# Inverse square root of the layer norms by Newton steps on VectorE, in a four-layer graph network

## The chip, the cores and the metric

The kernel runs on one core of a Trainium2 chip. A core has five engines that work side by side, each through its own instruction queue in order: TensorE (PE in the profile, with its weight loads as PEld), VectorE (DVE), ScalarE (ACT), GpSimd (POOL) and SyncE (SP, which here only starts transfers). They wait for each other by semaphores. The metric is the time of one execution on the device, in microseconds; several runs are made and their median is given. One further execution was recorded by the hardware profiler, and every view of the profile is of that one.

## The reference

Four layers run over 4096 nodes of 128 features and a 4096 x 4096 matrix `adj` that is mostly zero. Each layer first normalizes the rows and clips them at zero, computes a graph operation and adds the result to the rows.

```python
def _layernorm(x, axis=-1, eps=1e-5):
    m = jnp.mean(x, axis=axis, keepdims=True)
    v = jnp.var(x, axis=axis, keepdims=True)
    return (x - m) / jnp.sqrt(v + eps)

h = jnp.maximum(_layernorm(x, axis=-1), 0.0)
x = x + _L0_gnn_ref(h, adj, L0_gnn_W, L0_gnn_b)
h = jnp.maximum(_layernorm(x, axis=-1), 0.0)
x = x + _L1_gnn_ref(h, adj, L1_gnn_weight, L1_gnn_bias)
h = jnp.maximum(_layernorm(x, axis=-1), 0.0)
x = x + _L2_gnn_ref(h, adj, L2_gnn_weight, L2_gnn_att_src, L2_gnn_att_dst)
h = jnp.maximum(_layernorm(x, axis=-1), 0.0)
x = x + _L3_gnn_ref(h, adj, L3_gnn_msg_w, L3_gnn_msg_b, L3_gnn_upd_w, L3_gnn_upd_b, L3_gnn_ln_w, L3_gnn_ln_b)
```

The layers numbered 0 to 3 are these. Layer 0 multiplies by `adj` once and by two weights. Layer 1 multiplies by `adj` twice (a Chebyshev recursion). Layer 2 is an attention with `exp` over the nonzero places of `adj`. Layer 3 sends a message through a GELU for every nonzero place, sums the messages of a row weighted by `adj`, applies an update with another GELU and then a second layer norm of its own:

```python
        h = jax.nn.gelu(new_feats, approximate=False) + node_feats
        mu = jnp.mean(h, axis=-1, keepdims=True)
        var = jnp.var(h, axis=-1, keepdims=True)
        return (h - mu) / jnp.sqrt(var + LN_EPS) * ln_w + ln_b
```

## The kernel before

The rows lie in 32 blocks of 128 (a block is one row per partition), and four blocks make a group: there are eight groups, `NC`. The matrix is used as a list: the kernel reads `adj` once, marks its nonzero places (`mark`, a Sigmoid on ScalarE into an 8-bit mask), scans the masks on VectorE (`scan`), and builds lists of the rows and columns that each stripe of 256 needs. Blocks near the front of the ordering are dense and are multiplied as they are; the rest is gathered by indirect DMAs that GpSimd issues (`gather`, L552-L554). `entries` decodes the single nonzero places for layer 3.

The order of all this isn't written by hand. Every part is a Python generator that yields what it will need next: an engine with an estimated duration (`yield "DVE", 0.35`), a buffer from a set of slots, or an event. `Plan.run` picks, again and again, the part that could begin first, lets it emit its instructions and advances a clock for that engine. An activation that names a table (`on_act(n, "sqrt")`) costs 1.3 us more in the plan when the table last named was another one. At the end `in_order` fixes the order in which each engine's instructions came out. So an estimate that changes moves what stands beside it in all five queues. Gaps on TensorE which the plan foresees are filled with products of zeros (`fill`, L604-L610).

The layer norm in front of each layer is `norm` (L557-L580). It takes a `stat` tile with four rows of small numbers. VectorE sums each block's rows and scales the sum to minus the mean (L563, L564); ScalarE squares the centred rows with an accumulator, one block at a time, into a scrap tile `junk` (L568); ScalarE takes the square root of the variance plus `eps` (L572); VectorE takes the reciprocal and multiplies by minus the mean (L574, L575); ScalarE applies scale, bias and Relu block by block (L578). `norm` is called from four places: `begin` for two groups at a time (four calls with eight blocks each), `finish_0` and `finish_2` after layers 0 and 1 (eight calls each, four blocks), and `finish_3` after the attention (eight calls). That makes 28.

Layer 3's own norm is in `Messages.finish` (L1428-L1471), called once for each group. After the update's matmuls (L597) VectorE adds the bias (L1441), ScalarE applies the GELU (L1444), and VectorE adds the rows and forms the mean (L1447-L1449). Then come the same steps as in `norm`: squares (L1453), square root (L1456), reciprocal and product (L1458, L1459), and four Identity activations that scale the four blocks (L1462). VectorE multiplies by `ln_w` and adds the rows (L1466, L1467), and the group is stored. `ln_b` has been added to the rows earlier, at L1392.

Beside it in stage order, the parts that share the engines with these steps are: in the attention, `attend`, where ScalarE forms scores (L1229) and their `exp` (L1232), VectorE multiplies them by the matrix twice (L1236, L1238) and TensorE accumulates (L1253, L1255); in layer 2's preparation an `exp` of two columns (L1042); in layer 3, `prepare`, which runs a group's own rows through a GELU (`own`, L1377) and opens the group's sum (L1386), and `message`, where ScalarE and VectorE build a selection (L623, L625), VectorE a weight mask (L1403), TensorE the message's two terms (L1409, L1411), ScalarE its GELU (L1415), and TensorE adds it to the group's sum (L1421).

A second program, `dense_stack`, is there for matrices that the lists can't hold. It is behind a condition that does not hold for these inputs.

Of the kernel before, what the change touches and what calls it, by code (L numbers as in the profile page):

```python
# [18 lines left out]
I32 = mybir.dt.int32  # L19
AF = mybir.ActivationFunctionType  # L20
ALU = mybir.AluOpType
# [5 lines left out]
D = 128  # L27
P = 128
# [3 lines left out]
GB = BANK // D  # L32
HALF = N // 2
QUARTER = N // 4
EPS = 1e-5
# [331 lines left out]
def on_act(n, table=None):  # L367
    return ("ACT", 0.22 + 0.83e-3 * n) + ((table,) if table else ())
# [10 lines left out]
def sparse_stack(tc, x, adj, adjT, diag, w_self, w_neigh, b0, w1, b1, w2, att_src, att_dst,  # L379
# [7 lines left out]
    nc = tc.nc  # L387
    plan = Plan()
    EARLY = 7
    with ExitStack() as ctx:  # L390
# [7 lines left out]
        def kept(name, shape, dtype=F32):  # L398
            return keep.tile(list(shape), dtype, name=name, tag=name)
# [46 lines left out]
        nc.gpsimd.memset(ones, 1.0)  # L446
        ones8 = kept("ones8", (P, 1), F8)
        nc.gpsimd.memset(ones8, 1.0)
        eps = kept("eps", (P, 1))
        nc.gpsimd.memset(eps, EPS)  # L450

        def iota(name, shape, pattern, base=0, step=0, dtype=F32):
            t = kept(name, shape, dtype)
# [100 lines left out]
                                         in_offset=bass.IndirectOffsetOnAxis(ap=index, axis=0))  # L554


        def norm(blocks, dst):  # L557

            n = blocks.stop - blocks.start
            st = yield stats  # L560
            src = xN[:, blocks, :]
            yield on_dve(n * D)
            nc.vector.tensor_reduce(st[:, 0, :n], src, axis=AX.X, op=ALU.add)  # L563
            nc.vector.tensor_scalar_mul(st[:, 0, :n], st[:, 0, :n], -1.0 / D)  # L564
            junk = yield junks
            yield "ACT", 0.58 * n
            for k in range(n):
                nc.scalar.activation(junk, src[:, k, :], AF.Square, bias=st[:, 0, k:k + 1],  # L568
                                     accum_out=st[:, 1, k:k + 1])
            plan.release(junks, junk)  # L570
            yield on_act(n, "sqrt")
            nc.scalar.activation(st[:, 1, :n], st[:, 1, :n], AF.Sqrt, bias=eps, scale=1.0 / D)  # L572
            yield "DVE", 0.35
            nc.vector.reciprocal(st[:, 2, :n], st[:, 1, :n])  # L574
            nc.vector.tensor_mul(st[:, 3, :n], st[:, 0, :n], st[:, 2, :n])  # L575
            yield "ACT", 0.45 * n
            for k in range(n):
                nc.scalar.activation(dst[:, k, :], src[:, k, :], AF.Relu, scale=st[:, 2, k:k + 1],  # L578
                                     bias=st[:, 3, k:k + 1])
            plan.release(stats, st)  # L580
# [736 lines left out]
        class Messages:  # L1317
# [110 lines left out]
            def finish(self, g):  # L1428
                blocks = slice(g * GB, (g + 1) * GB)
                plan.release(s_tiles, self.s_rows[g])  # L1430
                agg = yield aggs
                yield on_act(BANK)
                nc.scalar.copy(agg, self.acc[g])
                plan.release(accs if g else picks, self.acc[g])
                p = yield banks
                yield "PE", 8 * 0.42
                times(p, GB, [(hT[:, g * BANK:(g + 1) * BANK], upd_h_sb), (agg, upd_a_sb)])
                plan.release(aggs, agg)
                f = yield f_tiles
                yield on_dve(BANK)  # L1440
                nc.vector.tensor_tensor(f, rows_of(p), by_block(upd_b_sb, GB), op=ALU.add)  # L1441
                plan.release(banks, p)
                yield on_act(BANK, "gelu")
                nc.scalar.activation(f, f, AF.Gelu)  # L1444
                st = yield stats
                yield "DVE", 1.5
                nc.vector.tensor_add(f, f, hA[:, blocks, :])  # L1447
                nc.vector.tensor_reduce(st[:, 0, :GB], f, axis=AX.X, op=ALU.add)
                nc.vector.tensor_scalar_mul(st[:, 0, :GB], st[:, 0, :GB], -1.0 / D)  # L1449
                junk = yield junks  # L1450
                yield "ACT", 0.58 * GB
                for k in range(GB):
                    nc.scalar.activation(junk, f[:, k, :], AF.Square, bias=st[:, 0, k:k + 1], accum_out=st[:, 1, k:k + 1])  # L1453
                plan.release(junks, junk)
                yield on_act(GB, "sqrt")
                nc.scalar.activation(st[:, 1, :GB], st[:, 1, :GB], AF.Sqrt, bias=eps, scale=1.0 / D)  # L1456
                yield "DVE", 0.35
                nc.vector.reciprocal(st[:, 2, :GB], st[:, 1, :GB])  # L1458
                nc.vector.tensor_mul(st[:, 3, :GB], st[:, 0, :GB], st[:, 2, :GB])  # L1459
                yield "ACT", 0.45 * GB  # L1460
                for k in range(GB):
                    nc.scalar.activation(f[:, k, :], f[:, k, :], AF.Identity, scale=st[:, 2, k:k + 1],  # L1462
                                         bias=st[:, 3, k:k + 1])
                plan.release(stats, st)
                yield "DVE", 1.4
                nc.vector.tensor_mul(f, f, by_block(ln_w_sb, GB))  # L1466
                nc.vector.tensor_add(f, f, xN[:, blocks, :])  # L1467
                yield SP
                nc.sync.dma_start(out_rows[:, blocks, :], f)
                plan.release(f_tiles, f, plan.transfer(P * BANK * 4) - 1)  # L1470
                self.through.set(plan.finish)  # L1471
# [526 lines left out]
```

## Time and profile before

| | |
|---|---|
| time, median of 3 runs | 1176.93 us (1172.99 to 1178.95) |
| the profiled execution, its own time | 1485.49 us |
| the profiled execution, span | 1483.4 us |
| mean granted TensorE clock in it | 0.842 |
| instructions | 19188 |
| moved by DMA | 236.03 MB, mean 159 GB/s |
| Square activations in `norm` (L568) | 128, 401 ns each |
| square roots (L572, L1456) | 36, 297 ns each |
| reciprocals (L574, L1458) | 32 with 128x4 elements, 173 and 178 ns each |
| Identity activations (L1462) | 32, 479 ns each |
| Relu activations (L578) | 128, 479 to 482 ns each |

The profiled execution is longer than the timed runs by 309 us, so a position in it (a microsecond from the start of the span) is not a position in a timed run. What can be carried over are durations of single instructions and the order in each queue, which is the same in every run.

A group of instructions in the profile is named by its line, engine and operation, and by what it writes and reads. After the bar stand the busy time and the mean duration of one in nanoseconds, and after the second bar the idle time of the engine just before them. Mean durations are given with start to end; neighbours overlap a little, so the distance from start to start can be smaller. In the chain of waits each entry has its start, its length and what ran: an engine with tile and line, or "issue" where the engine waited for nothing that the profile shows.

### The profile page before, as it was taken

How to read it: one execution, taken by the hardware profiler on the slowest of the kernel's cores; microseconds unless marked ns; L12 is line 12 of the kernel's file. 1: busy time of each engine (PE TensorE's matmuls, PEld its weight loads, DVE VectorE, ACT ScalarE, POOL GpSimd, SP SyncE). 2: the span in 40 equal slices, each digit the busy share in tenths (PEclk: the TensorE clock that was granted, in tenths of full speed). 3: DMA queues.
4: the chain of work that ended last, by engine and by line, in shares of the span. 5: the costliest groups of instructions: out<-in, count | busy, mean ns of one | idle time of the engine just before them, and what ended most of it. 6: DMA issues, size and time to landing. Idle time of an engine off the chain costs nothing.

```text
span 1483.4 us, 19188 instructions
## 1 busy us (share of the span) xinstructions
PE 1055.1 (71%) x5943; PEld 722.2 (49%) x5943; DVE 792.7 (53%) x2982; ACT 671.2 (45%) x1344; POOL 766.4 (52%) x832
## 2 busy tenths in 40 slices
PE   6786778877486687667677069968767872957774
PEld 2454556554265465455555045534434452645663
DVE  5796567787466476345645048444444451424453
ACT  5983466664021213113335048656555630334366
POOL 4136664344635565546656733765557346664530
PEclk9897799897697899778888579979888995988988
DMA  8999899895565777766544034333333212112210
GB/s 252 357 329 334 286 299 330 305 353 185 135 185 147 211 228 227 201 187 181 150 115 132 8 93 132 107 88 89 88 107 97 61 50 49 42 42 53 61 45 24
DMA packets 175415, 236.03 MB, mean 159 GB/s; under 512 B 22452, under 2 KB 155336, under 8 KB 167112
## 3 DMA queue, kind: packets, MB, share of 16 engines
q1 hardware_dynamic: 148904, 186.45, 37.8%
q0 software_dynamic: 26400, 48.27, 13.6%
q8 instruction: 49, 0.80, 0.2%
q14 instruction: 62, 0.51, 0.1%
HBM read 203.41 MB, written 31.23 MB: 158 GB/s over the span
## 4 chain that ended last, share of the span: by engine, by line
PE 23%; another core or an unknown queue 13%; ACT 10%; DVE 7%; issue 6%; DMA 1%; POOL 0%; ACTq 0%; SPq 0%; DVEq 0%; POOLq 0%
PE acc L1253 4%; PE acc L1255 3%; PE bank L597 2%; PE acc L1421 2%; PE acc L1139 2%; PE acc L1156 2%; ACT junk L1453 1%; ACT e L1229 1%; ACT junk L568 1%; PE bank L1411 1%; PE pick L610 1%; ACT e L1232 1%; PE bank L1409 1%; DVE ehit L891 1%
## 5 line engine op out<-in xcount | busy, mean ns | idle before, releaser
L553 POOL DMA_INDIRECT e_val<-in_adj,e_at x158 | 154.5, 978 | 48.0 <-issue 45.6
L553 POOL DMA_INDIRECT g<-h_tab,fetch_row x136 | 136.1, 1001 | 73.0 <-issue 34.3
L610 PE MATMUL pick<-nothing 128*128 128x512 f16 x536 | 142.9, 416 | 1.6 <-issue 1.6
L1139 PE MATMUL acc<-big,hA 128*128 128x256 f32 x448 | 131.7, 442 | 10.7 <-issue 7.7
L610 PEld LDWEIGHTS <-nothing 128*128 128x128 f16 x795 | 82.9, 107 | 99.3 <-issue 33.4
L553 POOL DMA_INDIRECT g<-a_tab,fetch_col x74 | 76.9, 1039 | 93.6 <-issue 45.3
L553 POOL DMA_INDIRECT rseg<-in_adjT,seg_row x68 | 71.1, 1046 | 103.4 <-issue 28.8
L1139 PEld LDWEIGHTS acc<-big,hA 128*128 128x128 f32 x448 | 96.4, 225 | 28.6 <-issue 9.5
L553 POOL DMA_INDIRECT cseg<-in_adj,seg_col x74 | 70.8, 957 | 63.9 <-issue 23.2
L891 DVE SCALAR_TENSOR_TENSOR ehit<-ehit,pos,pick 128x32 f32<-128x32 f32 (+7 forms) x158 | 38.8, 285 | 116.0 <-issue 80.1
L1236 DVE TENSOR_TENSOR tau<-e,big 128x512 f32<-128x512 f32 (+3 forms) x61 | 54.3, 891 | 85.5 <-ACT e L1232 47.8
L553 POOL DMA_INDIRECT g<-u_tab,fetch_row x68 | 64.6, 950 | 64.9 <-PE acc L1156 37.1
L888 ACT COPY ehit<-pick 128x192 f32<-128x192 f32 (+7 forms) x74 | 20.4, 286 | 154.5 <-remote 80.4
L553 POOL DMA_INDIRECT tau<-d_tab,e_col x63 | 60.6, 962 | 57.2 <-issue 15.0
L769 ACT ACTIVATE mask<-dst 128x2048 fp8e4<-128x2048 f32 x43 | 81.8, 1903 | 14.2 <-DMA dst<-in_adj 8.0
L553 POOL DMA_INDIRECT m<-d_tab,e_col x70 | 68.4, 977 | 38.5 <-issue 17.4
L1156 PE MATMUL acc<-big,g 128*128 128x256 f32 x272 | 80.2, 434 | 0.6 <-DMA big<-r_tab 0.5
L568 ACT ACTIVATE junk<-xN,stat 128x128 f32<-128x128 f32 x128 | 51.4, 401 | 60.0 <-DVE stat L564 27.0
L623 ACT ACTIVATE sel_t<-iota_row,mids 128x512 f32<-128x512 f32 (+3 forms) x43 | 27.1, 642 | 109.7 <-DVE mids L618 63.7
L610 PE MATMUL bank<-nothing 128*128 128x512 f16 x259 | 70.6, 414 | 2.7 <-issue 2.3
L884 PE MATMUL pick<-eA,esel 128*128 128x65 f16 (+7 forms) x158 | 27.0, 245 | 61.4 <-DVE esel L625 28.0
L1139 PE MATMUL acc<-big,hB 128*128 128x256 f32 x224 | 62.7, 420 | 1.7 <-DMA big<-in_adjT 1.7
(331 smaller groups left out, 2717.2 us busy)
## 6 DMA issues: line engine op xcount, KB each, us to landing
dst<-in_adj SPq DMA_DIRECT2D x43, 1024.0 KB
big<-in_adjT SPq DMA_DIRECT2D x45, 512.0 KB
raw<-in_adj SPq DMA_DIRECT2D x21, 1024.0 KB
big<-in_adjT SPq DMA_DIRECT2D x66, 256.0 KB
big<-r_tab SPq DMA_DIRECT2D x30, 512.0 KB
c_tab<-cseg SPq DMA_DIRECT2D x74, 128.0 KB
r_tab<-rseg SPq DMA_DIRECT2D x68, 128.0 KB
big<-c_tab SPq DMA_DIRECT2D x15, 512.0 KB
```

The costliest lines, as they stand in the source:

```text
L553: nc.gpsimd.indirect_dma_start(out=dst, out_offset=None, in_=table[:, :], in_offset=bass.IndirectOffsetOnAxis(ap=index, axis=0))
L568: nc.scalar.activation(junk, src[:, k, :], AF.Square, bias=st[:, 0, k:k + 1], accum_out=st[:, 1, k:k + 1])
L597: nc.tensor.matmul(p[:, k * D:(k + 1) * D], lhs[:, k * P:(k + 1) * P], w, start=i == 0, stop=i == len(terms) - 1)
L610: nc.tensor.matmul(idle[2][idle[1]], nothing[:, :P], nothing, start=True, stop=True)
L769: nc.scalar.activation(mask[:, h * HALF:(h + 1) * HALF], raw_of[b, h], AF.Sigmoid, scale=1e38, accum_out=marks[:, 2 * b + h:2 * b + h + 1] ...
L891: nc.vector.scalar_tensor_tensor(hit[:, q, :], hit[:, q, :], pos0[:, k + q:k + q + 1], pv[:, q, W:2 * W], op0=ALU.is_le, op1=ALU.mult, acc ...
L1139: nc.tensor.matmul(acc, self.near[:, b, :D], as_rows(t)[:, k, :], start=count == 0, stop=count == every - 1)
L1156: nc.tensor.matmul(acc, row[:, :D], r, start=count == 0, stop=count == every - 1)
L1236: nc.vector.tensor_mul(tau[:, :n, :], e[:, :n, :], a[:, :n, :])
L1253: nc.tensor.matmul(acc[0:1, CS:2 * CS], parts[k][:, D + 1:], tau[:, k, :], start=False, stop=False)
L1255: nc.tensor.matmul(acc[:, :CS], parts[k][:, :D], e[:, k, :], start=False, stop=self.count[s.index] == every - 1)
L1421: nc.tensor.matmul(acc[:, b % GB * P:(b % GB + 1) * P], m[:, q, :], r[:, q, :], start=False, stop=all(self.left[g * GB + k] == 0 for k in ...
```

## The change

`norm` and `Messages.finish` no longer take a square root on ScalarE and a reciprocal on VectorE. A new function `inverse_root` computes the inverse square root on VectorE alone: one operation for the variance plus `eps`, a shift and a subtraction on the number's bits for a first guess, and three Newton steps of three operations each. These are twelve operations on tiles of 128x4 (128x8 in `begin`), and each needs the result of the one before. The product with minus the mean that followed stays. In the planner's terms a step "ACT" with the table "sqrt" and a step "DVE" of 0.35 us become one step "DVE" of 1.6 us. The constant `eps` and its memset go.

In `Messages.finish` the first two of a group's four blocks are scaled by ScalarE as before, and the last two by VectorE with a `tensor_scalar` of the same two operands.

```diff
--- before.py
+++ after.py
@@ -446,8 +446,6 @@
         nc.gpsimd.memset(ones, 1.0)
         ones8 = kept("ones8", (P, 1), F8)
         nc.gpsimd.memset(ones8, 1.0)
-        eps = kept("eps", (P, 1))
-        nc.gpsimd.memset(eps, EPS)
 
         def iota(name, shape, pattern, base=0, step=0, dtype=F32):
             t = kept(name, shape, dtype)
@@ -554,6 +552,17 @@
                                          in_offset=bass.IndirectOffsetOnAxis(ap=index, axis=0))
 
 
+        def inverse_root(st, n):
+
+            v, y, t = (st[:, k, :n] for k in (1, 2, 3))
+            nc.vector.tensor_scalar(v, v, 1.0 / D, EPS, op0=ALU.mult, op1=ALU.add)
+            nc.vector.tensor_scalar(y.bitcast(I32), v.bitcast(I32), 1, None, op0=ALU.logical_shift_right)
+            nc.vector.tensor_scalar(y.bitcast(I32), y.bitcast(I32), -1.0, float(0x5f3759df), op0=ALU.mult, op1=ALU.add)
+            for _ in range(3):
+                nc.vector.scalar_tensor_tensor(t, y, -0.5, y, op0=ALU.mult, op1=ALU.mult)
+                nc.vector.tensor_mul(t, t, v)
+                nc.vector.scalar_tensor_tensor(y, t, 1.5, y, op0=ALU.add, op1=ALU.mult)
+
         def norm(blocks, dst):
 
             n = blocks.stop - blocks.start
@@ -568,10 +577,8 @@
                 nc.scalar.activation(junk, src[:, k, :], AF.Square, bias=st[:, 0, k:k + 1],
                                      accum_out=st[:, 1, k:k + 1])
             plan.release(junks, junk)
-            yield on_act(n, "sqrt")
-            nc.scalar.activation(st[:, 1, :n], st[:, 1, :n], AF.Sqrt, bias=eps, scale=1.0 / D)
-            yield "DVE", 0.35
-            nc.vector.reciprocal(st[:, 2, :n], st[:, 1, :n])
+            yield "DVE", 1.6
+            inverse_root(st, n)
             nc.vector.tensor_mul(st[:, 3, :n], st[:, 0, :n], st[:, 2, :n])
             yield "ACT", 0.45 * n
             for k in range(n):
@@ -1452,15 +1459,17 @@
                 for k in range(GB):
                     nc.scalar.activation(junk, f[:, k, :], AF.Square, bias=st[:, 0, k:k + 1], accum_out=st[:, 1, k:k + 1])
                 plan.release(junks, junk)
-                yield on_act(GB, "sqrt")
-                nc.scalar.activation(st[:, 1, :GB], st[:, 1, :GB], AF.Sqrt, bias=eps, scale=1.0 / D)
-                yield "DVE", 0.35
-                nc.vector.reciprocal(st[:, 2, :GB], st[:, 1, :GB])
+                yield "DVE", 1.6
+                inverse_root(st, GB)
                 nc.vector.tensor_mul(st[:, 3, :GB], st[:, 0, :GB], st[:, 2, :GB])
-                yield "ACT", 0.45 * GB
-                for k in range(GB):
+                yield "ACT", 0.45 * (GB // 2)
+                for k in range(GB // 2):
                     nc.scalar.activation(f[:, k, :], f[:, k, :], AF.Identity, scale=st[:, 2, k:k + 1],
                                          bias=st[:, 3, k:k + 1])
+                yield "DVE", 0.3 * (GB // 2)
+                for k in range(GB // 2, GB):
+                    nc.vector.tensor_scalar(f[:, k, :], f[:, k, :], st[:, 2, k:k + 1], st[:, 3, k:k + 1],
+                                            op0=ALU.mult, op1=ALU.add)
                 plan.release(stats, st)
                 yield "DVE", 1.4
                 nc.vector.tensor_mul(f, f, by_block(ln_w_sb, GB))
```

## The prediction

> **What bounds the kernel now.** I read the page's totals first, then each engine by stage, then ScalarE's groups, then the chain of work that ended last. The totals and the stages:
>
> ```profile
> PE 1055.1 (71%) x5943; PEld 722.2 (49%) x5943; DVE 792.7 (53%) x2982; ACT 671.2 (45%) x1344; POOL 766.4 (52%) x832
> ...
> 0.00:412.00 412.00, 302.52 (x2184) 194.50 (x2185) 286.66 (x932) 238.85 (x395) 193.82 (x244) 0.85 0.84 285
> 412.00:882.00 470.00, 309.45 (x1581) 240.13 (x1579) 241.90 (x1342) 122.92 (x300) 270.93 (x287) 0.81 0.56 161
> 882.00:1184.00 302.00, 244.99 (x1053) 135.15 (x1054) 142.41 (x301) 190.18 (x395) 162.08 (x158) 0.89 0.35 96
> ```
>
> The stage rows give start:end, length, then the busy time of PE, weight loads, DVE, ACT and POOL, the clock, the DMA share and GB/s. I call them A (layer 0, the scan of the matrix), B (layers 1 and 2), C (attention) and D (messages, from 1184 to the end). In A the DMA engines are 84% busy: transfers set the pace. No engine fills B to D; there the order of waits decides.
>
> ScalarE's groups, shapes kept apart, show where its function tables are loaded:
>
> ```profile
> L572 ACT ACT_TABLE_LOAD x26 | 33.4, 1283 | 0.5
> L769 ACT ACT_TABLE_LOAD x10 | 12.8, 1283 | 0.2
> L1232 ACT ACT_TABLE_LOAD x8 | 10.3, 1283 | 0.1
> L1456 ACT ACT_TABLE_LOAD x8 | 10.3, 1283 | 0.1
> L1042 ACT ACT_TABLE_LOAD x7 | 9.0, 1283 | 0.1
> L1377 ACT ACT_TABLE_LOAD x6 | 7.7, 1283 | 0.1
> ```
>
> With three at L1415 and one each at L1444 and L1482 there are 70 loads of 1283 ns: 89.8 us, 13% of ScalarE's busy time. 34 are the square roots' own (L572, L1456); most others bring back the table that a square root displaced.
>
> The chain in D, at one `finish` (start, length, what):
>
> ```profile
> 1411.07 0.49 ACT junk L1453 x2
> 1411.56 0.02 issue
> 1411.58 1.28 ACT L1456
> 1412.86 0.01 issue
> 1412.88 0.30 ACT stat L1456
> 1413.17 0.02 issue
> 1413.19 1.28 ACT L1377
> 1414.47 0.01 issue
> 1414.48 0.64 ACT own L1377
> 1415.12 0.04 issue
> 1415.17 2.08 PE acc L1386 x8
> ```
>
> An ACT entry with a line and no tile is a table load. The next group's GELU (`own`, L1377) needs nothing of this square root; it stands behind it in ScalarE's order, and TensorE waits for it. Load, root and reload cost that path 1.30 + 0.32 + 1.30 = 2.92 us with their issue gaps.
>
> I added up such entries over the whole chain, which this view resolves from 579 us on (none in A). A load begun as 0.04 plus "issue" of about 1.2 counts as one. B: 6 loads, 7.7 us. C: 12 loads, 15.0 us. D: 16 loads, 20.4 us. Together 43 us.
>
> **What the Trainium skill says.** *ScalarE: Activation LUTs*, What ACT_TABLE_LOAD costs: 1283 ns a load for every set, plus about 1380 ns of drain. The 1283 is the trace's to the nanosecond; the drain is not: the root starts 1.29 us after its load starts, so I price a load at 1.30. The same page, Table sets: sqrt, exp, sigmoid and gelu anchor different sets, relu, copy, abs and identity are in every one. The trace agrees: no load stands at the Relu (L578), the copies (L590) or the Abs (L623). *VectorE: DVE Perf Modes*, The TRN2 errata: a fixed cost per instruction, for a float32 two-tensor operation (N+151)/0.96 ns; for 4 elements an estimate of 161 ns, and L1459 took 163. *SBUF — State Buffer*, Who interferes with whom: VectorE operations with two SBUF inputs or in a two-port mode lock a port that GpSimd shares[...]. All twelve new operations are of these kinds; the trace speaks on both sides, below.
>
> **The change part by part.**
>
> *Removed from ScalarE.* 36 square roots (28 at L572, 8 at L1456) of 0.297 us: 10.7 us. The loads: after the change only sigmoid, exp and gelu need tables, and these come nearly in this order by stage. I keep one each, a return to exp after the first early GELU in C, and a few alternations: 6 to 10 of 70. So about 62 loads or 79.5 us go. The 16 identities that leave L1462 (0.385 us from start to start) are 6 us. ACT falls from 671 to about 575.
>
> *Added to VectorE.* Twelve operations for each of 36 norms, each needing the one before. A dependent chain of such small operations runs at 0.213 us per step with POOL idle:
>
> ```profile
> 658.32 0.18 DVE L922 TENSOR_TENSOR da<-da,db 128x22 int32<-128x22 int32 x1
> 658.53 0.18 DVE L921 TENSOR_SCALAR db<-dv 128x22 int32<-128x22 int32 x1
> 658.75 0.18 DVE L922 TENSOR_TENSOR da<-da,db 128x22 int32<-128x22 int32 x1
> 658.96 0.18 DVE L921 TENSOR_SCALAR db<-dv 128x22 int32<-128x22 int32 x1
> ```
>
> 12 x 0.213 = 2.56 us, against the reciprocal's 0.21: 2.35 us more a norm, 85 us of the queue's time in all (some 70 busy). DVE goes from 793 to about 867, the 16 moved blocks at 0.28 included. Where the norm's own result is waited for, the path had 1.30 + 0.32 + 0.21 = 1.83 and gets 2.56: 0.73 us longer.
>
> *D.* Three chain passages go through `own` as above: 3 x 2.92 = 8.8. Three go through the scaling (L1462), which began 3.45 us after the last `junk` (1328.55 to 1332.00). It can now begin after 2.56 + 0.21 = 2.77, and ScalarE does two blocks in 0.87 instead of four in 1.63: 3 x (0.68 + 0.76) = 4.3. At 1465 the last GELU (L1444) stands behind load, root and reload: 2.92. The last norm loses 0.73 and gains 0.76 in its scaling: nothing. One root of a norm at 1196 gives 1.6. Sum 17.6. The two blocks on VectorE lie beside ScalarE's two; without that cover they cost 0.56. What is behind the twelve operations on DVE: masks and selections of the next messages (L1403, L625), for which TensorE waits at L1421 and L1411. DVE is 43% busy there and covers them; uncovered they cost 8 x 2.35 = 19 us.
>
> *C.* 15.0 + 5 roots at 0.32 = 16.6 if all comes off. But after the loads at 955, 1072 and 1149 the chain runs into waits of 16.0, 11.7 and 9.3 us which the profile gives to an unknown queue. Time saved ahead of such a wait may only lengthen it. Bounds 0 and 16.6; I take half, 8.3. Behind the twelve operations stand the products of the attention (L1236, L1238) that feed L1253 and L1255.
>
> *B.* 7.7 + 0.3, less 2.35 where the norm at 893 is followed by its own use: 5.7. After three of the five loads at L1042 an unknown wait follows (6.6, 15.1, 2.4 us). Bounds 0 and 5.7; I take 2.5.
>
> *A.* 22 loads and 12 roots, 32 us of ScalarE, lie under the DMA. Only at the start (17 to 35 us) was ScalarE busy without a break ahead of the first mask, so the reads start up to 2.9 us sooner: I take 2. DVE gets 28 us more on 287 of 412; if that holds up the scan it costs, so bounds 8 won and 8 lost.
>
> *Sum.* 17.6 + 8.3 + 2.5 + 2 = 30.4; I give back 5 for what queues behind the DVE blocks (bounds 0 and 36, the blocks of C and D all uncovered): 25 us. The removed `eps` constant is one small memset on POOL: nothing. The planner lays out all five queues anew from the changed costs, so neighbours move everywhere; I add no mean for that, only spread, some 10 us either way (a choice, not a reading).
>
> **Against the profile's own time.** The profiled execution took 1485.49 us, its span 1483.4, which leaves 2.1 around it; with the change it would take about 1460. The timed runs' median is 1176.93, 309 less. The chain's unknown waits and issue from 579 on come to 198 + 95 us, near that, but nothing shows that they are the difference. The loads have one fixed duration, so I carry the 25 us over in microseconds: 1152.
>
> **The rivals.**
>
> *All of it counts.* If the unknown waits are shorter in timed runs, B and C come off whole: 17.6 + 16.6 + 5.7 + 8 and 4 for a better order in D, 52 us: 1125. For it: the 309 us. Against it: TensorE is 81% busy in C.
>
> *Absorbed.* The waits of B and C end where they ended, and the DVE blocks eat most of D: 3 us remain, 1174. For it: the waits that follow the loads. Against it: the passages of D, where TensorE waits for ScalarE directly.
>
> *VectorE's chain stalls on POOL (slower).* In one burst of gathers small operations were held for a gather's period of 1.25 us each:
>
> ```profile
> 817.60 0.16 DVE L848 SCALAR_TENSOR_TENSOR middle<-efirst,half 128x4 f32<-128x4 f32 x1 [1.08 <-DVE half L847]
> 818.99 0.17 DVE L849 TENSOR_TENSOR mids<-middle,shift 128x12 f32<-128x12 f32 x1 [1.23 <-DVE middle L848]
> ```
>
> A norm there costs 12 x (1.25 - 0.213) = 12.4 us more. It decides from two norms on the path (25 / 12.4); with four it gives 1152 + 50 = 1202. Against it: from 695 to 700 POOL was 75% busy and a like chain still took 0.21 us a step.
>
> **How the numbers follow.** Forecast 0.50 (own range 1137 to 1166), all of it 0.20, absorbed 0.17, stall 0.13. A measurement here can tell about 0.5%, 6 us, from none. Faster: 0.50 + 0.20 + 0.07 of the absorbed case = 0.77; same 0.10; slower 0.13. The range 1122 to 1182 leaves out the stall's upper part and the far end of the second case, under 0.2 in all.
>
> **What would show it.** Right: 6 to 10 loads in all and none behind a `junk`, ACT near 575 and DVE near 867, `own` following `junk` at once in D, and a norm's twelve steps in about 2.6 us. Wrong: those steps spread over 5 us or more, TensorE waiting for L1403, L625 or L1236 behind them, or the unknown waits of C longer by what was saved.

## The result, and the profile after

The change made a difference of a few us at most: 1176.22 us against 1177.15 us for the kernel before (medians of 20 runs each on one chip), ratio 0.9983, 95% interval 0.9963 to 1.0003. A second comparison, on another chip, gave 1174.98 us against 1178.90, ratio 0.9972 (0.9948 to 0.9996). The forecast of 1152 us was wrong; "absorbed", at 1174, came nearest. Medians here and below are of all runs, while ratios and their intervals leave out runs well above the fastest of the same kernel, so that the two can differ by some tenths of a per cent.

One fact has to stand ahead of every reading. There are chips on which the kernel before took 1470 to 1555 us in every run, with mean granted TensorE clocks of 0.816 to 0.845. The profile that the prediction read (1485.49 us, clock 0.842) looks like one of these, though which chip it came from isn't on record; the times are from chips on which the kernel takes 1177 us. All profiles below are of the second kind unless the text says otherwise, and so the kernel before is shown here from a profile of its own there (span 1175.5 us).

The page of the changed kernel, totals and slices (a slice is 29.5 us):

```profile
PE 986.2 (84%) x5853; PEld 677.7 (57%) x5853; DVE 863.2 (73%) x3394; ACT 575.7 (49%) x1228; POOL 773.1 (66%) x831
...
PE   5888787888788898888888879889999978778783
...
DVE  6799898878878887675898866666567672356785
ACT  4985556655522212231434456577677642234552
POOL 5127746545437677777777777777777777777770
```

The same of the kernel before, on a chip of the same kind:

```profile
PE 985.6 (84%) x5943; PEld 675.0 (57%) x5943; DVE 792.2 (67%) x2982; ACT 673.5 (57%) x1344; POOL 769.7 (65%) x832
...
PE   5977988898788888787898789898999988887892
...
DVE  5789988889878758567877756465546482455563
ACT  4997667676523131231556486477778761255676
POOL 5115777435546777777777778777777747777760
```

And the POOL row of the page that the prediction had before it:

```profile
POOL 4136664344635565546656733765557346664530
```

ScalarE lost 98 us of work and VectorE gained 71, as forecast, and neither shows in the time. Look at POOL. From the fourteenth slice on both rows say 7 almost throughout, and 7 looks like slack. It isn't. A gather is recorded for 0.94 us, the next begins 0.30 us after its end for "issue", and 0.94 of 1.25 is 7 tenths: a row of sevens is a full queue. In the third row there are sixes, fives, fours and threes, pauses that this kernel has only on the other kind of chip.

TensorE's share needs a caution too. It includes the products of zeros with which the plan fills gaps (L610 before, L617 after): 208 of the 985.6 us before and 185 of the 986.2 us after.

ScalarE's groups in the changed kernel hold all table loads that are left, six, one to a line; two of them:

```profile
L776 ACT ACT_TABLE_LOAD x1 | 1.3, 1283 | 0.0
L1049 ACT ACT_TABLE_LOAD x1 | 1.3, 1283 | 0.0
```

VectorE's timeline at one norm of `finish_3`, changed kernel (start, length):

```profile
952.52 0.19 DVE L558 TENSOR_SCALAR stat<-stat 128x4 f32<-128x4 f32 x1
952.76 0.17 DVE L559 TENSOR_SCALAR stat<-stat 128x4 int32<-128x4 int32 x1
952.97 0.19 DVE L560 TENSOR_SCALAR stat<-stat 128x4 int32<-128x4 int32 x1
953.20 0.16 DVE L562 SCALAR_TENSOR_TENSOR stat<-stat 128x4 f32<-128x4 f32 x1
...
955.00 0.16 DVE L582 TENSOR_TENSOR stat<-stat 128x4 f32<-128x4 f32 x1
```

Twelve operations from 952.52 to 955.00 are 2.48 us; 2.56 had been worked out. Over all 36 norms of this profile they take 2.37 to 2.62 us. The single operations of the Newton steps take 164 ns (L562 to L564, 96 of each at four elements), where 161 had been estimated. The parts of the change were priced right. What bounds the kernel was not.

**Where the time lies.** GpSimd's gathers come in the same number in every kernel that keeps them (595 after the last gather of row segments, `rseg`), so they serve as marks. I cut the span at the start of that last `rseg` gather and at the first gather of `tau`, the message rows that need the attention's result complete: its last part must have been stored in the table `d_tab` first. GpSimd's timeline, kernel before:

```profile
350.78 0.95 POOL L553 DMA_INDIRECT rseg<-in_adjT,seg_row  x1 [0.30 <-PE pick L657]
...
956.37 0.93 POOL L553 DMA_INDIRECT e<-d_tab,e_col  x1 [0.30 <-ACT junk L568]
968.48 0.95 POOL L553 DMA_INDIRECT tau<-d_tab,e_col  x1 [11.18 <-DVE n_bad L1524]
...
1142.00 0.92 POOL L553 DMA_INDIRECT e<-d_tab,e_col  x1 [0.30 <-issue]
```

The changed kernel:

```profile
365.17 0.95 POOL L551 DMA_INDIRECT rseg<-in_adjT,seg_row  x1 [0.30 <-PE pick L664]
...
928.41 1.26 POOL L551 DMA_INDIRECT g<-a_tab,fetch_col  x1 [0.30 <-issue]
929.98 0.94 POOL L551 DMA_INDIRECT e_val<-in_adj,e_at  x1 [0.30 <-DVE e_val L953]
...
943.93 0.95 POOL L551 DMA_INDIRECT e_val<-in_adj,e_at  x1 [0.30 <-issue]
...
969.34 0.94 POOL L551 DMA_INDIRECT e<-d_tab,e_col  x1 [0.30 <-issue]
970.59 0.94 POOL L551 DMA_INDIRECT tau<-d_tab,e_col  x1 [0.30 <-issue]
...
1148.92 0.92 POOL L551 DMA_INDIRECT e<-d_tab,e_col  x1 [0.31 <-issue]
```

The brackets give the idle time before the entry and what ended it. So part 1 (A and a little less) ends at 350.8 and 365.2 us, part 2 (B and C) lasts 617.7 and 605.4 us, part 3 (D) 207.0 and 209.0 us. The prediction's profile, cut the same way, has 387.3, 820.6 and 275.5: of the 308 us between it and the kernel before at 1177 us, 271 lie in parts 2 and 3.

In part 2 the kernel before has a pause of 11.2 us at its end; the changed one has none. In both, some 33 us pass from the attention's last gather (`g<-a_tab`, at 932.8 before and 928.4 after) to the start of the last store into `d_tab` (965.6 and 962.3), which must land before `tau`. The old order left 18 gathers for that stretch, 22 us of GpSimd's work. The new one leaves 32, since twelve gathers of edge values, which the old order had put earlier, now stand after the attention's last gather. So the attention's gathers are also served sooner: its last one starts 582 us after the last `rseg` before, 563 us after it now.

A second profile of the changed kernel (span 1165.9 us) has 350.9, 606.6 and 208.5. The 13.7 us between the two lie in part 1 alone; parts 2 and 3 differ by 0.6 us in sum over some 815 us. I use that as a tool: the sum of parts 2 and 3 is read from one profile, and part 1, which scatters, is the median time less that sum (some 2 us around the span included). That the sum repeats so well rests on this one pair; on the slower chips three profiles of the kernel before have 1085, 1096 and 1104 us.

### The profile page after: what moved, and what is told of

It is laid out like the page before. It is cut to its first block, busy times and chain, and to the rows that moved or that the text cites. A ratio compares the mean times of both kernels' runs of the same rounds, so it can differ in the third digit from the quotient of the medians.

```text
span 1179.6 us, 19316 instructions
## 1 busy us (share of the span) xinstructions
PE 986.2 (84%) x5853; PEld 677.7 (57%) x5853; DVE 863.2 (73%) x3394; ACT 575.7 (49%) x1228; POOL 773.1 (66%) x831
## 5 line engine op out<-in xcount | busy, mean ns | idle before, releaser
L551 POOL DMA_INDIRECT e_val<-in_adj,e_at x158 | 159.1, 1007 | 48.0 <-issue 41.6
L1146 PE MATMUL acc<-big,hA 128*128 128x256 f32 x448 | 121.1, 413 | 3.0 <-DMA big<-in_adjT 3.0
L617 PEld LDWEIGHTS <-nothing 128*128 128x128 f16 x705 | 71.8, 104 | 79.8 <-issue 19.8
L617 PE MATMUL pick<-nothing 128*128 128x512 f16 x435 | 117.5, 417 | 0.0
L1146 PEld LDWEIGHTS acc<-big,hA 128*128 128x128 f32 x448 | 88.1, 207 | 15.4 <-DMA big<-in_adjT 3.8
L551 POOL DMA_INDIRECT m<-d_tab,e_col x79 | 78.4, 992 | 24.1 <-issue 13.7
L1163 PE MATMUL acc<-big,g 128*128 128x256 f32 x272 | 75.0, 407 | 7.6 <-DMA big<-r_tab 4.4
L551 POOL DMA_INDIRECT tau<-d_tab,e_col x67 | 66.7, 996 | 20.4 <-issue 11.9
L617 PE MATMUL bank<-nothing 128*128 128x512 f16 x270 | 67.1, 385 | 0.0
L1163 PE MATMUL acc<-rseg,g 128*128 128x256 f32 x136 | 51.9, 490 | 13.1 <-DMA g<-h_tab,fetch_row 13.1
L1163 PEld LDWEIGHTS acc<-big,g 128*128 128x128 f32 x272 | 50.9, 200 | 18.8 <-issue 7.9
```

Of the source, the lines that this page charges most:

```text
L551: nc.gpsimd.indirect_dma_start(out=dst, out_offset=None, in_=table[:, :], in_offset=bass.IndirectOffsetOnAxis(ap=index, axis=0))
L617: nc.tensor.matmul(idle[2][idle[1]], nothing[:, :P], nothing, start=True, stop=True)
L1146: nc.tensor.matmul(acc, self.near[:, b, :D], as_rows(t)[:, k, :], start=count == 0, stop=count == every - 1)
L1163: nc.tensor.matmul(acc, row[:, :D], r, start=count == 0, stop=count == every - 1)
```

## The experiments

**On a chip like that of the first profile.** Four kernels ran on one of the slower chips, where the kernel before takes 1483.12 us (median of 23). The kernel before once more:

> The kernel before once more, for a profile beside which the changed kernel's can be laid (its own profile had a span of 1483 us, the changed one's 1180). Theory (GpSimd's queue): GpSimd issues its 736 gathers without a pause from about 400 us on, one each 1.25 us, and the last one starts between 1140 and 1155 us, as in the changed kernel (1149); the table loads are there (70) and hidden beside it. Rival (the gain was given back on VectorE): here GpSimd has pauses of more than 20 us in sum after 400 us, and waits for ScalarE show in the chain.

1470.12 us, span 1468.1: the profile that was predicted from is no outlier there. The theory failed on this chip: after the last `rseg` GpSimd pauses for some 260 us in sum, as the rival said.

The kernel before and the changed kernel, each without the 158 gathers of edge values (the values that layer 3's messages take from the matrix are left out):

```diff
-                        gather(e_val[:n, k:k + 1], adj_flat, e_at[:n, k:k + 1])
```

> The kernel before, the order of all other instructions held, without the 158 gathers of matrix values (the values of layer 3's messages are left out, their weights are zero). Theory (GpSimd's queue): 158 x 1.25 = 197 us leave the queue that sets the time, so the time falls by 60 to 197 us, until something else is the bound. Rival (VectorE gave the gain back; GpSimd is not the bound): within 15 us of the kernel before.

> The changed kernel, the order of all other instructions held, without the same 158 gathers (the values of layer 3's messages are left out). Theory (GpSimd's queue): falls as the kernel before does without them, and now that GpSimd no longer covers it the change shows: 8 to 30 us faster than the kernel before without them. Rival (given back on VectorE): the two are within 5 us of each other, or this one is slower.

1335.39 us, ratio 0.9042 (0.8961 to 0.9122), and 1330.36 us, 0.8988 (0.8926 to 0.9051). Some 150 us go in both, and without these gathers the two still differ by no more than 5 us, which is what the rival said and not the theory. More gathers, 28 of them issued twice into the same place, in the changed kernel:

```diff
                         gather(e_val[:n, k:k + 1], adj_flat, e_at[:n, k:k + 1])
+                        if number >= 5 and k % 3 == 0:
+                            gather(e_val[:n, k:k + 1], adj_flat, e_at[:n, k:k + 1])
```

> The changed kernel with 28 of its value gathers (those of the later row groups, issued after about 550 us) issued twice, everything else in the same order. Theory (GpSimd's queue): 28 x 1.25 = 35 us more in a queue without pauses, so 25 to 35 us slower. Rival: under 10 us slower, since GpSimd is busy for 66% of the span and has room.

1496.38 us, ratio 1.0074 (1.0044 to 1.0105) to the kernel before, 11 us more, which lies nearer the rival (the changed kernel wasn't run there without the doubled gathers). Little can be concluded from this chip for the 1177 us, but gathers weigh there too.

**The parts of the change, on chips with 1177 us.** The changed kernel again:

> The changed kernel once more, beside the kernel before and the other runs of this call on one chip. On the chip of the last call the kernel before took 1483 us instead of 1177. Theory (gathers on GpSimd, or what waits for them, set the time; ScalarE's loads lie beside them): ratio to the kernel before 0.985 to 1.005 wherever it runs. Rival (the prediction's path of loads counts where the chip is the slower one): 0.965 to 0.985 there.

1174.98 us, as above; on this chip the kernel before takes 1178.90. Then the loads alone, on the same chip: the kernel before in its old order, with an Identity where the square root stood and nothing added to VectorE (the root itself is left out; the same edit is made in `Messages.finish`):

```diff
-            nc.scalar.activation(st[:, 1, :n], st[:, 1, :n], AF.Sqrt, bias=eps, scale=1.0 / D)
+            nc.scalar.activation(st[:, 1, :n], st[:, 1, :n], AF.Identity, bias=eps, scale=1.0 / D)
```

> The kernel before in its own order, with the square root activation replaced by an Identity of the same size (the root is left out, the rows are scaled by the reciprocal of the variance): no square root table, so about 64 of the 70 loads go, and VectorE gets nothing in return. Theory (loads lie beside the gathers): less than 10 us faster. Rival 1 (the loads were on the path and VectorE's twelve operations gave the gain back): 20 to 45 us faster. Rival 2 (the new order gave it back): also 20 to 45 us faster.

1165.36 us against 1178.90, ratio 0.9855 (0.9796 to 0.9914): 64 of the 70 loads are worth 13.5 us by the medians, 10 to 24 by the interval (four runs). That is more than the theory allowed, by the median less than both rivals asked for, and less than the 30.4 that had been added up. Then the twelve operations in the old order, with the old durations left in the plan and all four scalings on ScalarE (the same edit in `Messages.finish`):

```diff
             yield on_act(n, "sqrt")
-            nc.scalar.activation(st[:, 1, :n], st[:, 1, :n], AF.Sqrt, bias=eps, scale=1.0 / D)
             yield "DVE", 0.35
-            nc.vector.reciprocal(st[:, 2, :n], st[:, 1, :n])
+            inverse_root(st, n)
```

> The twelve operations on VectorE in place of root and reciprocal, but with the planner's old estimates, so that every queue keeps the order of the kernel before (the scaling of the blocks is unchanged). Theory: within 8 us of the kernel before. Rival 1 (VectorE gives it back): within 8 us too, but then noload_before is 20 us or more faster than this. Rival 2 (the new order cost what the loads gave): 15 to 40 us faster than the kernel before and than the changed one.

1181.01 us, ratio 1.0017 (0.9997 to 1.0036). The same order with loads off and operations on is 15.6 us slower than with loads off alone. So in the old order the operations take back what the loads give. Then the changed kernel with six Newton steps, in the changed order:

```diff
-            for _ in range(3):
+            for _ in range(6):
```

> The changed kernel with six Newton steps instead of three, everything else in the same order: nine more dependent operations for each of 36 norms, 9 x 0.21 = 1.9 us each, 69 us of VectorE's queue. Theory (VectorE lies beside the gathers): up to 10 us slower. Rival 1 (VectorE's queue gave the gain back): 20 to 60 us slower than the changed kernel.

1196.98 us, ratio 1.0154 (1.0104 to 1.0204): 22 us for nine more operations in each norm, which is in the range of the first rival and over the theory's. VectorE's operations do cost, and more than was "given back".

**Where they cost.** The kernel before for a profile of its own:

> The kernel before, once more, for its profile beside those of its relatives with the same order. If GpSimd's queue of gathers sets the pace from about 400 us on, its gathers stand 1.25 us apart there with next to no pauses, as in the changed kernel, and the kernel that has no square root in this order starts its gathers earlier by an amount that is reached in the first 400 us and doesn't grow after. If the order of waits decides in B to D, GpSimd pauses, and the lead of the kernel without roots grows through B, C and D to its 13.5 us.

1177.31 us; its lines are shown above. GpSimd has next to no pause from 400 us on apart from the 11.2 us ahead of `tau`. The lead of the kernel without roots is 6.3 us at the last `rseg`, 7.6 us at the first `tau` and 5.8 us at the last gather: it hardly changes in between, although ScalarE has 22 us less to do from 400 to 850. The first theory's expectation holds up to there; its "next to no pauses" overlooked the one of 11 us, and after the last gather, where GpSimd no longer sets the pace, the lead grows by 4.8 us to 10.6 (these are single profiles).

Two steps in place of three:

> The changed kernel with two Newton steps in place of three (six fewer ... three fewer operations in each norm, nine in place of twelve). If what VectorE's operations cost is paid in A (a slope of 2.4 us per operation added to every norm, from the kernel with six steps), three operations less give 5 to 8 us: about 1169. If the operations are hidden, no change: 1175. If VectorE's chain counts at each of the 36 norms, 36 x 3 x 0.21 = 23 us: 1152.

1168.59 us, ratio 0.9912 (0.9877 to 0.9947): 7 us faster than the changed kernel, as the slope from six steps said, and far from the 23 us of a chain that counts at every norm. That the gain lies in A is not confirmed: by the table below about half of it does. Then the roots of layer 0 (`begin` and `finish_0`, in part 1, which set the flag `early`) back on ScalarE, with their loads:

```diff
-            yield "DVE", 1.6
-            inverse_root(st, n)
+            if early:
+                yield on_act(n, "sqrt")
+                nc.scalar.activation(st[:, 1, :n], st[:, 1, :n], AF.Sqrt, bias=eps, scale=1.0 / D)
+                yield "DVE", 0.35
+                nc.vector.reciprocal(st[:, 2, :n], st[:, 1, :n])
+            else:
+                yield "DVE", 1.6
+                inverse_root(st, n)
```

> The changed kernel, but the norms of layer 0 (in A, lines of begin and finish_0) take their root from ScalarE again, with its table loads; all other norms have the Newton steps. If VectorE's added operations in A cost 10 us and the table loads of A cost less, it is 4 to 10 us faster than the changed kernel: 1165 to 1171. If the loads of A cost as much as the operations there, no change: 1175. If the loads of A cost more (ScalarE's share of the scan), it is slower: 1180 to 1185.

1168.21 us, ratio 0.9911 (0.9874 to 0.9947), 7 to 8 us faster than the changed kernel. Parts 2 and 3 take 813.7 us, as in the changed kernel (814.4); the gain is part 1's. So in part 1 the change loses. Whether the operations themselves or the new order lose there this run doesn't tell, since the edit puts back the plan's old estimates too; in the old order the change lost nothing in part 1 (table below).

**Whether GpSimd's queue is full.** The doubled gathers again:

> The changed kernel with 28 gathers of edge values issued twice into the same place, 28 x 1.25 us = 35 us more of GpSimd's queue and nothing else of note. If GpSimd's queue sets the pace, 28 to 35 us slower: 1203 to 1210. If the order of waits decides, under 10 us slower: up to 1185.

1258.25 us, ratio 1.0689 (1.0633 to 1.0745): 82 us more, over every expectation. The waits of GpSimd explain the size:

```profile
POOL e_val L551 <- DMA e_val<-in_adj,e_at: 54.1, 29, 3.7
```

(total us, times, longest.) The second gather writes where the first does and waits until that has landed. In the changed kernel this row has 2.1 us in seven entries of 0.3, the usual distance. So 28 x 1.25 = 35 us of gathers and 54.1 - 29 x 0.3 = 45 us of waiting beyond that distance, 80 us in all, were put into GpSimd's queue, and 82 arrive at the end. Nothing else had slack to take it up.

Then the other direction, the 158 gathers of edge values taken out of the changed kernel:

> The changed kernel without its 158 gathers of edge values (the values that layer 3's messages take from the matrix are left out). 158 x 1.25 = 197 us of GpSimd's queue go. If that queue sets the pace from 400 us on, 120 to 197 us go, until TensorE (84% of the span busy) sets it: 980 to 1055. If the order of waits of the other engines decides, under 30 us go: over 1145.

1149.97 us, ratio 0.9775 (0.9732 to 0.9817). 197 us left the queue and only 26 us came off (33 by the parts of its profile, all of them in part 2), under everything that the theory of one full queue had asked for, and what its rival allowed. The stretch from 700 to 900 us shows why. Changed kernel, then the kernel without these gathers (length, then busy PE, weight loads, DVE, ACT, POOL, the clock, DMA share, GB/s):

```profile
700.00:900.00 200.00, 186.28 (x820) 103.92 (x820) 128.63 (x311) 136.61 (x298) 155.66 (x151) 0.97 0.45 124
```

```profile
700.00:900.00 200.00, 197.96 (x897) 111.41 (x895) 141.69 (x325) 152.97 (x336) 91.59 (x88) 1.00 0.47 137
```

POOL falls from 156 to 92 us, and TensorE, at 186 of 200, goes to 198. Behind the full queue stood TensorE with 7% to spare in its given order, in which some 10 us of either figure are products of zeros. This kernel also has the pause ahead of `tau` back:

```profile
POOL tau L551 <- DMA d_tab<-agg: 19.6, 1, 19.6
```

So part 2 is a near tie of three: the gathers, TensorE's attention, and the chain that must finish before `tau`. Lengthening the gathers counted in full; shortening them did little. The other two weren't lengthened by themselves.

Fewer gathers with everything computed, two steps and the columns planned for less gathering:

```diff
-R_EXTRA, C_EXTRA = 2, 1.5
+R_EXTRA, C_EXTRA = 2, 2
```

> The kernel with two Newton steps, and the columns' stripes planned at a price of 2 in place of 1.5 for each gathered block: 68 gathered blocks in place of 74, each with two gathers (its table rows and its matrix segments), so 12 gathers less, and 18 whole blocks more, which TensorE multiplies. If GpSimd's queue sets the pace from 400 us on, 12 x 1.25 = 15 us go, less what VectorE and TensorE need more: 1153 to 1163 against 1169 with two steps. If it doesn't, TensorE's added work shows: 1168 to 1180.

1169.25 us, ratio 0.9936 (0.9911 to 0.9962): nothing against two steps alone, as the second expectation had it. Twelve gathers of 1.25 us went, and GpSimd's waits from 900 us have this in their place:

```profile
POOL tau L551 <- DMA d_tab<-agg: 11.5, 1, 11.5
```

15 us off the queue, 11.2 us more waiting at the gate of part 3. The run isn't a clean test, since the plan was made anew: all gathers of edge values stand ahead of the attention's last gather again, which has 427 gathers between the last `rseg` and itself, against 425 with two steps alone. The attention was not served sooner, and only 19 gathers are left for the stretch ahead of `tau`, so that the pause is back.

**What took the pause away in the changed kernel.** The changed kernel without its second edit, four scalings on ScalarE:

```diff
-                yield "ACT", 0.45 * (GB // 2)
-                for k in range(GB // 2):
+                yield "ACT", 0.45 * GB
+                for k in range(GB):
...
-                yield "DVE", 0.3 * (GB // 2)
-                for k in range(GB // 2, GB):
-                    nc.vector.tensor_scalar(f[:, k, :], f[:, k, :], st[:, 2, k:k + 1], st[:, 3, k:k + 1],
-                                            op0=ALU.mult, op1=ALU.add)
```

> The changed kernel with the second edit undone: all four blocks of a group of layer 3 scaled by ScalarE. In the kernel before, and in those of its order, GpSimd's queue pauses 11 us before the first gather of tau, behind a VectorE operation, and in the changed kernel it doesn't. If the new order of the work that came with the new durations removed that pause, it is gone here too and this kernel is as fast as the changed one: 1172 to 1178. If the second edit removed it, the pause is back and this is 6 to 10 us slower: 1181 to 1186.

1176.39 us, ratio 0.9990 (0.9969 to 1.0011), no pause (0.3 us ahead of `tau`): the new order removed it, as the first expectation said, and the second edit is worth nothing that can be measured in the time.

**The best of both.** Two steps, and ScalarE's roots in layer 0:

> The kernel with ScalarE's roots in layer 0, and two Newton steps instead of three in the other norms. Measured so far: with ScalarE's roots in layer 0 the part up to the last gather of row segments takes about 354 us, with two steps the part after it takes 810 us (815 with three). If the two parts add up, 1164 to 1166, the fastest of the kernels that compute everything. If the two steps gained only in layer 0, as the theory that B to D hide VectorE's operations has it, no change against the kernel with ScalarE's roots there and three steps: 1168.

1513.19 us against 1526.89, ratio 0.9931 (0.9889 to 0.9972): this came from another of the slower chips. So did a further profile of the kernel before, 1500.61 us, so that its parts 2 and 3 at 1177 us rest on one profile:

> The kernel before once more, for a second profile of it: the part after the last gather of row segments should again take about 825 us (824.7 in the profile at hand), with GpSimd's pause of 11 us before the first gather of tau, if the part from there on is set by fixed queues; the part before it may differ by 10 us and more from 351.

Once more, and this time where the kernel before takes 1177.88 us:

> The same kernel as hybrid2, for a time beside those of 1177 us of the kernel before. If the two parts add up: 1164 to 1166. If two steps gain only in layer 0: 1168.

1166.38 us, ratio 0.9904 (0.9869 to 0.9939), the lowest of the kernels that compute everything, though within the intervals of the kernels with one of the two edits. The time doesn't decide between 1164 to 1166 and 1168; parts 2 and 3, at 809.7 us, are those of two steps (810.1), as adding up asks.

All kernels by parts, in us. "2 + 3" is read from the profile; part 1 is the median less that.

| kernel | time | part 1 | part 2 | part 3 | 2 + 3 |
|---|---|---|---|---|---|
| before | 1177.3 | 352.6 | 617.7 | 207.0 | 824.7 |
| loads off, old order | 1165.4 | 345.0 | 616.4 | 204.0 | 820.4 |
| twelve operations, old order | 1181.0 | 352.4 | 619.4 | 209.2 | 828.6 |
| twelve operations, new order | 1176.4 | 361.9 | 607.2 | 207.3 | 814.5 |
| changed | 1176.2 | 361.8 | 605.4 | 209.0 | 814.4 |
| two steps | 1168.6 | 358.5 | 601.6 | 208.5 | 810.1 |
| six steps | 1197.0 | 372.6 | 610.4 | 214.0 | 824.4 |
| ScalarE's roots in layer 0 | 1168.2 | 354.5 | 604.6 | 209.1 | 813.7 |
| the same, two steps | 1166.4 | 356.7 | 602.1 | 207.6 | 809.7 |
| two steps, fewer gathers | 1169.3 | 352.4 | 606.6 | 210.3 | 816.9 |

From line to line, part 1 and then 2 + 3: the loads give 7.6 and 4.3 us, the operations take 7.4 and 8.2, the new order takes 9.5 and gives 14.1, the second edit does nothing. The sum is 9 us lost in part 1 and 10 won after it. The differences in part 1 carry the scatter of medians, some 2 us each and more where the runs are few, and that of the chips: the rows come from chips on which the kernel before takes 1177.2 to 1178.9 us. Measured on one chip, the loads give 13.5 us in all, so 9 in part 1, and the changed kernel's part 1 there is 360.0, so that the new order and the second edit take 8.

Part 3 can be cut once more, at the last gather, which starts at 1142.0 us in the kernel before:

| kernel | first `tau` to last gather | last gather to the end |
|---|---|---|
| before | 173.5 | 33.5 |
| loads off, old order | 175.3 | 28.7 |
| twelve operations, old order | 176.8 | 32.5 |
| twelve operations, new order | 175.7 | 31.7 |
| changed | 178.3 | 30.7 |
| six steps | 179.0 | 35.0 |

While GpSimd gathers in D, taking the loads off gives nothing; in the 30 us without gathers it gives 4.8, and the twelve operations take 3.8 of them back.

## Why the prediction was wrong

- **The step that failed** is the first: "No engine fills B to D; there the order of waits decides." On the chips that were timed GpSimd's queue fills B to D up to the last gather: 595 gathers at 1.25 us are 744 of 791 us, pauses are 19 and most of the rest is gathers that took longer, and TensorE is up to 93% busy close behind. Such a stretch passes on little of what a table load on ScalarE saves: with the loads off, parts 2 and 3 gained 4.3 us, where 28.4 had been summed for the whole edit. The claim was a right reading of a profile that wasn't of the timed kernel's time.
- **The chain's loads.** In D the time from the first `tau` gather to the last gather is 173.5 us before and 178.3 after, for 137 and 138 gathers; 137 x 1.25 = 171. ScalarE's passages through `own` lie beside that queue. Only what follows the last gather (1142.0 and 1148.9) could shorten: from 33.5 to 30.7 us. The end of the kernel before has these passages, in the chain of waits:

```profile
1157.23 1.28 ACT L1456
1158.53 0.30 ACT stat L1456
1158.84 1.28 ACT L1444
1160.13 0.64 ACT f L1444
...
1164.54 1.28 ACT L1456
1165.84 0.31 ACT stat L1456
```

  The 2.8 us that came look like the 2.92 forecast for load, root and reload ahead of the last GELU, but the likeness is chance. With the loads off this end was 4.8 us shorter, the twelve operations took 3.8 back, and the new order and the second edit gave 1.8.
- **Stage A.** "In A the DMA engines are 84% busy: transfers set the pace" was half of it. The windows of the kernel before from 100 to 300 us:

```profile
100.00:200.00 100.00, 85.81 (x693) 61.71 (x693) 86.29 (x252) 69.25 (x104) 75.69 (x74) 0.88 1.03 385
200.00:300.00 100.00, 88.23 (x719) 58.38 (x720) 85.88 (x230) 68.81 (x101) 51.16 (x49) 0.86 0.98 358
```

  DMA is full, and VectorE is 86% busy beside it (TensorE too, but 60 of its 174 us are products of zeros). The bounds were 8 won and 8 lost; 9 were lost, just outside, so that "I take 2" had the wrong sign. The runs with other numbers of steps show that VectorE's operations reach part 1: from two steps to six, 14 us there.
- **The give-back.** 5 us were taken, with bounds of 0 and 36; the operations cost 15.6 us in the old order, about half of it in part 1. From two steps to six 14 us fall in parts 2 and 3 as well, and of the 10 from three to six there 4 lie after the last gather and 5 are a new wait for `d_tab` ahead of `tau`. The twelve operations themselves ran as priced.
- **The second edit**, 4.3 us in D: nothing that shows in the time, probably for the same reason as the loads.
- **The new order**, "no mean for that, only spread, some 10 us either way": 4.6 us won in all, but as 9.5 lost and 14.1 won, each as large as most of what was priced. Twelve gathers moved behind the attention's last one go with the pause that went, 11 of the 14 us, and the edit wasn't about them. They weren't moved alone.
- **Counts and busy times** were right: six loads left (6 to 10), ACT 575.7 (about 575), DVE 863.2 (about 867). What *ScalarE: Activation LUTs*, Table sets, says of which functions share a set carried the count of loads, and the trace agrees with its six.
- **The rivals.** "Absorbed" had 3 us left at 1174: right in time, and half right in cause, so partly by luck. It had the waits of B and C end where they ended and VectorE's blocks eat D. In fact GpSimd's queue hid most of the gain in B to D, VectorE's cost fell in A as much as after it, and two shifts of the new order that nobody had priced nearly cancelled. "VectorE's chain stalls on POOL" did not happen: with GpSimd gathering one after another, a step took 0.21 us, and no norm took over 2.62.
- **Carrying the 25 us over in microseconds** was the choice that let the error through. The profile stood 309 us above the median, and the text said that nothing showed what the difference was. Most of it, 271 of 308 us, was in the waits that B to D seemed to be made of.

Not settled: why the new order costs 8 to 9.5 us in part 1 (it wasn't tried alone, without the operations), how much of its gain in part 2 is due to the moved gathers, and what makes GpSimd pause, and the kernel take 300 us more, on some chips, where the changed kernel itself was not timed. The granted clock is about 10% lower there, while the time is 26% longer and more.

## What to carry to other kernels

Before pricing an edit, compare the profile's own time with the median; here they stood a quarter apart and the profile's waits weren't those of the timed kernel, so that what is built on such slack needs a wide range or a case of its own. Read an engine's busy share together with the gap that follows each of its instructions: GpSimd showed 75% here and had no free place. Ask also how much of a busy share is filling. Where several queues are within some per cent of one another, ask of each edit which queue it shortens and how far the next one is behind: here 80 us added to one queue cost 82, and 197 taken away gave 26.

## What the runs showed of the hardware

- A gather issued by GpSimd mostly occupies its queue for 1.25 us (0.94 recorded, 0.30 to the next), and the next one doesn't wait for the data to land unless it writes to the same place. *Perfetto Trace Analysis*, DMA Instruction — SWDGE (GPSIMD), says that the recorded interval ends when the descriptors are made, not when the data land. The trace agrees: in the doubled gathers the next one waited up to 3.7 us for a landing.
- The same program took 1169 to 1185 us on some chips and 1470 to 1555 us on others, in every run made there, with mean granted TensorE clocks of 0.920 to 0.952 and 0.816 to 0.845. GpSimd's row is full in one and has pauses in the other.
- A chain of twelve dependent small VectorE operations took 2.37 to 2.62 us in all 36 norms, beside full gathering or not.
- Two executions of the changed kernel that differ by 13.7 us differ in the first 365 us; the following 815 us repeat to 0.6 us.
